# Layer 1's sums of a two-layer graph attention kernel: two column-tiled rounds in a row instead of one

## The chip, the cores and the metric

The kernel runs on one core of a Trainium2 chip. Its engines work side by side and meet at semaphores: TensorE (PE; its weight loads are a row of their own, PEld), VectorE (DVE), ScalarE (ACT), GpSimd (POOL, which here issues the gathers) and SyncE (SP, which issues most other transfers). Sixteen DMA engines move the data. The metric is the device time of one execution in microseconds (us), lower is better.

## The reference, cut to what matters

3125 nodes with 768 features each, 53,125 edges sorted by destination, two graph attention layers. The first one has 4 heads of 256 columns, the second one head of 768.

```python
h = jnp.maximum(_layernorm(x), 0.0)
def gat_conv(x, edge_index, W, a_src, a_dst, bias, heads, out_ch, concat):
    xl = (x @ W).reshape(n, heads, out_ch)
    ...
    e = jax.nn.leaky_relu(alpha_src[src] + alpha_dst[dst], 0.2)
    m = jax.ops.segment_max(e, dst, num_segments=n)
    e = jnp.exp(e - m[dst])
    s = jax.ops.segment_sum(e, dst, num_segments=n)
    alpha = e / (s[dst] + 1e-16)
    msg = xl[src] * alpha[:, :, None]
    out = jax.ops.segment_sum(msg, dst, num_segments=n)
...
h = gat_conv(x, edge_index, W1, a_src1, a_dst1, b1, HEADS, HID, True)
h = jax.nn.relu(layer_norm(h, g1, be1)) + (h0 @ Wr1 + br1)
h1 = h
h = gat_conv(h, edge_index, W2, a_src2, a_dst2, b2, 1, OUT_DIM, False)
h = layer_norm(h, g2, be2) + (h1 @ Wr2 + br2)
```

The change lies in layer 1's last sum: for each node, the rows `xl[src]` of its edges, each times its weight, added up.

## The kernel before

All is float32 in this part. The products of layer 1 are written to a table in HBM, 1024 columns (4 KB) a row. Destination nodes are worked on in 25 blocks (`NB`) of 128, the last of 53. The edges of a block lie in up to 17 tiles (`J`) of 128 slots. A tile serves one quarter of the block's nodes, 32 of them, and three tiles serve two quarters (`QUARTERS`).

`sums` (line 703) does the sum. For each tile, one indirect DMA on POOL gathers the 128 source rows into a buffer `g` (512 KB, line 774; `ahead` = 13 buffers in layer 1). DVE builds the columns `w` (lines 800 and 801): for each head a matrix of 128 slots by 32 nodes, with the edge's weight where slot and node belong together. TensorE multiplies `w` (as weights, 32 columns) with 256 columns of `g` and adds in PSUM (`pa`, line 821). A matmul with 32 columns uses a quarter of the array, and the output's quarter of the partitions says which. So tiles of different quarters are taken together: `ROUNDS` (line 33) has five rounds of 4, 4, 3, 3 and 3 tiles for a block, and within a round the four quarters follow one another for each 256 columns. Each float32 matmul is two instructions, and a round has 4 x 4 x 2 = 32. A buffer of `g` is free when its round has ended.

Between the rounds other work is done, one step after each round (`step(k)`, line 714), in this order:

- the next piece of `first()` (line 1198), which at the start finishes the totals of the weights, stores them, and loads `W2`;
- the next piece of each block that is being finished (`finish`, line 725, and `end1`, line 1207): three steps of waiting (`lag`), then normalisation on DVE and ACT, eight transposes on TensorE (line 1229), bias, gain, ReLU and residual on ACT and DVE (1234, 1236), a store of `h1T`, 12, 12 and 8 products with `W2` (line 1250) in three steps, copies of these from PSUM (1255 on ACT, 1257 on DVE) and a store to the table of layer 2. The transposes and these products share the two PSUM buffers `p2`;
- `pace[k]` pieces of `later()` (line 1170), the product `h0 @ Wr1` for 13 of the blocks in six groups. A piece is two matmuls (four instructions, line 1181); three pieces fill one `pr` buffer in PSUM (two of them), which ACT empties (line 1188). Its input `h0k` is loaded column block by column block for the next group as the last row of products of a group is done (`load`, line 1160; 11 buffers). A group waits while more than four blocks of it would stand unfinished, and for that time there are no pieces.

The order on PE, ACT and DVE is the order in which the program writes the instructions; SP and POOL take theirs as a scheduler lists them, and wait in that order for buffers. After the matmuls of a round, `fetch` (line 767) issues the next round's gathers, `w`, the load of the block's own rows (`own`, SP) and the small lookup of the totals (`ao`, POOL), and then comes the step. Layer 2 calls the same `sums` (line 1364) with one head of 768 columns and 26 buffers.

Of the kernel before, what the change touches and what calls it, by code (L numbers as in the profile page):

```python
# [9 lines left out]
F32 = mybir.dt.float32  # L10
# [58 lines left out]
def in_order(  # L69
# [16 lines left out]
    nc = tc.nc  # L86
# [5 lines left out]
    P = 128  # L92
# [23 lines left out]
    def rows_of(b):  # L116
        return P if b < NB - 1 else LAST
# [582 lines left out]
        nc.vector.tensor_scalar(ends[:, :, :, 1], al, -1.0, None, op0=OP.is_ge)  # L700
        nc.vector.scalar_tensor_tensor(ends[:, :, :, 2], eo, 2.0, ends[:, :, :, 1], op0=OP.mult, op1=OP.mult)

    def sums(heads, cols, table, al, alo_d, ahead, lag, gp, pp, end, more, pace, first=None):

        width = heads * cols
        f = width // 2
        n = min(cols, f)  # L710
        running = []
        due = 0.0

        def step(k):
            nonlocal due
            next(first or iter(()), None)
            for g in list(running):
                if next(g, running) is running:
                    running.remove(g)
            due += pace[k]  # L720
            while due >= 1.0:
                due -= 1.0
                next(more, None)

        def finish(b, own, pa):
            for _ in range(lag):
                yield

            r = rows_of(b)
            share = None  # L730
            if heads == 1:
                at = pa[:r, 1, f:f + 3]
                v = gp.tile([P, 4], F32, name="v", bufs=2)[:r]
                nc.vector.tensor_scalar(v[:, 0:1], at[:, 1:2], 0.1, 2.0, op0=OP.is_lt, op1=OP.mult)
                nc.vector.tensor_scalar(v[:, 1:2], at[:, 1:2], 0.1, None, op0=OP.max)
                nc.vector.reciprocal(v[:, 1:2], v[:, 1:2])
                nc.vector.scalar_tensor_tensor(v[:, 2:3], at[:, 2:3], v[:, 1:2], v[:, 0:1], op0=OP.mult, op1=OP.add)
                nc.vector.tensor_scalar(v[:, 3:4], at[:, 0:1], v[:, 2:3], 1e-16, op0=OP.add, op1=OP.add)
# [12 lines left out]
            for o in range(0, width, n):  # L751
                nc.vector.scalar_tensor_tensor(z[:, o:o + n], own[:r, o:o + n], aw[:r, o // cols:o // cols + 1],  # L752
                                               pa[:r, o // f, o % f:o % f + n], op0=OP.mult, op1=OP.add)
            yield from end(b, z, share)

        asked = {}

        def ask(b):
            ao = asked[b] = gp.tile([128, 2 * heads, NB], F32, name="ao", bufs=3)
            nc.gpsimd.indirect_dma_start(  # L760
                out=ao.rearrange("p v b -> p (v b)"), out_offset=None, in_=alo_d[:, :],
                in_offset=bass.IndirectOffsetOnAxis(ap=at_last[:, b:b + 1], axis=0))

        extra = 3 if heads == 1 else 0
        owns = {}

        def fetch(b, k):

            got = {}
            for j in ROUNDS[k]:  # L770
                if j >= tiles_of(b):
                    continue
                g = gp.tile([128, width + extra], F32, name="g", bufs=ahead)
                nc.gpsimd.indirect_dma_start(  # L774
                    out=g[:, :width], out_offset=None, in_=table[:, :],
                    in_offset=bass.IndirectOffsetOnAxis(ap=idx_s[:, b * J + j:b * J + j + 1], axis=0))
                if heads == 1:
                    nc.scalar.activation(g[:, width:], alo_d[:, POS[j], b, :], AF.Copy)
                got[j] = g, weights_of(b, j)
                count = PLACE[j]  # L780
                if count == 4:
                    own = owns[b] = gp.tile([128, width], F32, name="own", bufs=3)
                    load_rows(nc.sync, own, table, b)
                if heads > 1 and b == 1 and count == 11:
                    ask(0)
                if heads > 1 and b and count == (13 if tiles_of(b) == J else 5):
                    ask(b)
            return got

        def weights_of(b, j):  # L790

            c = b * J + j
            lo, hi = 32 * QUARTERS[j][0], 32 * QUARTERS[j][-1] + 32
            w = gp.tile([128, heads, hi - lo], F32, name=f"w{hi - lo}", bufs=9 if hi - lo == 32 else 3)
            if heads == 1:
                nc.vector.tensor_scalar(w[:, 0, :], iota_f[:, lo:hi], rel_s[:, c:c + 1], al[:, POS[j], 0, b:b + 1],  # L796
                                        op0=OP.is_equal, op1=OP.mult)
            else:
                oh = gp.tile([128, 64], F32, name="oh", bufs=4)[:, :hi - lo]
                nc.vector.tensor_scalar(oh, iota_f[:, lo:hi], rel_s[:, c:c + 1], None, op0=OP.is_equal)  # L800
                nc.vector.tensor_tensor(w, oh[:, None, :].to_broadcast([128, heads, hi - lo]),  # L801
                                        al[:, POS[j], :, b:b + 1].to_broadcast([128, heads, hi - lo]), OP.mult)
            return w

        with tc.manual_schedule(engines={PE, ACT, DVE}):
            ready = fetch(0, 0)
            for b in range(NB):
                pa = pp.tile([P, 2, 512], F32, name="pa", bufs=2)
                opened = set()
                last_q = (rows_of(b) - 1) // 32  # L810
                for k, js in enumerate(ROUNDS):
                    made = []
                    for j, (g, w) in ready.items():
                        for i, q in enumerate(QUARTERS[j]):
                            if q <= last_q:
                                made.append((q, w[:, :, 32 * i:32 * i + 32], g))
                    for o in range(0, width, n):
                        for q, w, g in made:
                            to = (o // f, q)
                            m = n + (extra if o + n == width else 0)  # L820
                            nc.tensor.matmul(pa[32 * q:32 * q + 32, o // f, o % f:o % f + m], w[:, o // cols, :],  # L821
                                             g[:, o:o + m], start=to not in opened, stop=False,
                                             skip_group_check=True)
                            opened.add(to)
                    if k + 1 < len(ROUNDS):
                        ready = fetch(b, k + 1)
                    elif b + 1 < NB:
                        ready = fetch(b + 1, 0)
                    step(k)
                running.append(finish(b, owns.pop(b), pa))  # L830
            k = 0
            while running:
                step(k)
                k = (k + 1) % len(ROUNDS)


    with tc.tile_pool(name="m1", bufs=1) as mp:
# [318 lines left out]
        with tc.tile_pool(name="w2", bufs=1, reuse_waits="tile") as wp, tc.tile_pool(name="e1", bufs=2, reuse_waits="tile") as ep, \  # L1156
# [3 lines left out]
            def load(i, k, q=nc.sync):  # L1160
                if i < NG:
                    n = cols_of(i)
                    t = loaded[i, k] = wp.tile([128, WIDE], F32, name="h0k", bufs=11)
                    q.dma_start(t[:, :n], h0T_d[i][:, k, :n])

            for k in range(NK1):
# [31 lines left out]
            def first():  # L1198
                nonlocal w2
                yield from totals(H, al1, alo1, alo1_d, keep1, xs1, pp, "p2", 2)  # L1200
                yield
                w2 = mp.tile([128, NK2, R2], F32, tag="W", name="w2")
                for k in range(NK2):
                    nc.sync.dma_start(w2[:, k, :C2], W2[k * 128:(k + 1) * 128, :])
                nc.vector.tensor_copy(w2[:, :, C2:], wa2)
# [51 lines left out]
                        nc.vector.tensor_copy(asad2[:r, b, :], pm[:, 384:n])  # L1257
                store_rows(nc.sync, table2, b, row)

            sums(H, C1, table1, al1, alo1_d, 13, 3, gp, pp, end1, more, (2.5, 3.8, 0, 0, 0.9), first())  # L1260


    with tc.tile_pool(name="m2", bufs=1, reuse_waits="tile") as mp, \
# [573 lines left out]
```

## Time and profile before

| what | us |
|---|---|
| three runs | 1987.45, 1987.87, 1988.3 (median 1987.87) |
| the profiled execution | 1979.75 |
| its span, from the first instruction to the last | 1977.9 |
| layer 1's sums, first and last matmul of line 821 | 514.7 and 1241 |

The profile is of one execution. A line of the groups gives the line of the kernel, the engine, the operation with output and inputs, the count, then the busy time, the mean in ns of one, and the idle time of the engine before these instructions with what ended it. A line of the timeline gives start, duration and the merged instructions, and in brackets the idle time before. The ends of matmuls are modelled, so differences between starts say more than durations. DMA share is the mean busy share of the sixteen DMA engines, and packets that overlap bring it a little above 1.

### The profile page before, as it was taken

What the parts mean: (1) busy time and instruction counts of PE and PEld (TensorE: products, weight loads), DVE (VectorE), ACT (ScalarE), POOL (GpSimd) and SP (SyncE); (2) the same over time, 40 slices, a digit from 0 to 9 for tenths busy, and PEclk for the clock granted to TensorE, in tenths of its full rate; (3) what the DMA queues carried; (4) which work ended last, traced back from release to release, by engine and by line L of the source; (5) the groups of instructions that cost most, each with busy time, mean ns of one, the idle gap of its engine ahead of it and who ended that gap; (6) DMA issues with size and microseconds to landing.
All of it is one profiled execution on the core that took longest, in us unless ns stands there. A gap on an engine that the chain in (4) does not pass through costs nothing. (4 is left out here: it accounts for less than half of the span.)

```text
span 1977.9 us, 34115 instructions
## 1 busy us (share of the span) xinstructions
PE 1805.4 (91%) x12558; PEld 985.3 (50%) x12558; DVE 1062.9 (54%) x3030; ACT 296.8 (15%) x1094; POOL 905.6 (46%) x969
## 2 busy tenths in 40 slices
PE   6999999998779999999989998878889998998886
PEld 4666665665445655655555554464333333333332
DVE  7672536888445556555665564443444443444446
ACT  1121431001202211211211121101000000000000
POOL 2000101110455666656656663006666666666663
PEclk9999999999889999999998999978999999999999
DMA  6833537872799999999999996588999999999984
GB/s 211 290 102 119 142 111 220 184 175 61 274 409 366 389 402 379 405 345 402 397 375 388 383 355 248 166 282 289 317 331 331 336 328 326 330 334 329 329 302 166
DMA packets 180978, 574.87 MB, mean 291 GB/s; under 512 B 32767, under 2 KB 54265, under 8 KB 180676
## 3 DMA queue, kind: packets, MB, share of 16 engines
q0 software_dynamic: 107472, 403.57, 57.4%
q1 hardware_dynamic: 69802, 159.43, 23.3%
q10 hardware_dynamic: 3530, 9.60, 1.2%
q8 instruction: 103, 1.69, 0.3%
q14 instruction: 71, 0.58, 0.1%
HBM read 503.27 MB, written 73.85 MB: 292 GB/s over the span
## 5 line engine op out<-in xcount | busy, mean ns | idle before, releaser
L774 POOL DMA_INDIRECT g<-table,idx_s x832 | 824.7, 991 | 511.8 <-issue 205.6
L821 PE MATMUL pa<-g,w 128*32 128x256 f32 (+2 forms) x5868 | 551.4, 430 | 91.6 <-issue 67.7
L821 PEld LDWEIGHTS pa<-g,w 128*32 128x32 f32 x5868 | 207.9, 111 | 399.5 <-issue 277.4
L1289 PE MATMUL pr<-wr,h 128*128 128x384 f32 (+1 forms) x800 | 295.7, 508 | 15.0 <-issue 14.4
L1250 PE MATMUL p<-w,h1T 128*128 128x384 f32 (+2 forms) x800 | 281.9, 499 | 4.0 <-DVE h1T L1236 2.6
L796 DVE TENSOR_SCALAR w<-iota_f,rel_s,al 128x32 f32<-128x32 f32 (+1 forms) x416 | 105.1, 321 | 311.6 <-PE pa L821 210.4
L1289 PEld LDWEIGHTS pr<-wr,h 128*128 128x128 f32 (+1 forms) x800 | 143.6, 191 | 169.3 <-issue 100.8
L1250 PEld LDWEIGHTS p<-w,h1T 128*128 128x128 f32 (+1 forms) x800 | 144.8, 189 | 127.9 <-issue 34.7
L801 DVE TENSOR_TENSOR w<-oh,al 128x128 f32<-128x128 f32 (+1 forms) x416 | 132.1, 317 | 129.2 <-PE pa L821 82.2
L924 PE MATMUL pm<-w,h0l 128*128 128x344 f32 (+1 forms) x468 | 142.5, 459 | 0.0
L1181 PE MATMUL pr<-h0k,wr 128*128 128x256 f32 (+1 forms) x576 | 140.7, 391 | 1.3 <-issue 1.3
L924 PE MATMUL pm<-w,h0g 128*128 128x344 f32 x432 | 131.0, 459 | 1.6 <-ACT h0g L903 1.6
L1059 PE MATMUL pm<-h0g,wr 128*128 128x512 f32 x288 | 131.7, 605 | 0.0
L1181 PEld LDWEIGHTS pr<-h0k,wr 128*128 128x128 f32 x576 | 105.9, 190 | 30.7 <-issue 11.8
L992 POOL DMA_DIRECT2D hot_d<-ohd x25 | 13.5, 540 | 225.3 <-DVE own L502 131.1
L800 DVE TENSOR_SCALAR oh<-iota_f,rel_s 128x32 f32<-128x32 f32 (+1 forms) x416 | 112.3, 270 | 0.3 <-issue 0.2
L924 PEld LDWEIGHTS pm<-w,h0l 128*128 128x128 f32 (+1 forms) x468 | 85.6, 187 | 45.0 <-issue 7.1
L491 ACT ACTIVATE bn_sd<-bn_mv,eps 128x1 f32<-128x1 f32 (+1 forms) x50 | 14.7, 294 | 611.6 <-DVE bn_mv L487 401.8
L924 PEld LDWEIGHTS pm<-w,h0g 128*128 128x128 f32 x432 | 81.9, 193 | 42.1 <-ACT h0g L903 1.8
L1059 PEld LDWEIGHTS pm<-h0g,wr 128*128 128x128 f32 x288 | 53.4, 193 | 56.5 <-issue 56.4
L1234 ACT ACTIVATE h1T<-p,be_c,g_c 128x128 f32<-128x128 f32 (+1 forms) x200 | 72.0, 474 | 16.7 <-PE p L1229 9.5
L551 PEld LDWEIGHTS <-ohs 128*128 128x128 bf16 x1275 | 59.7, 97 | 14.3 <-issue 14.3
(304 smaller groups left out, 1407.6 us busy)
## 6 DMA issues: line engine op xcount, KB each, us to landing
s<-slo_d SPq DMA_DIRECT2D x25, 544.0 KB
g<-table,idx_s POOLq DMA_INDIRECT x832
table<-row SPq DMA_DIRECT2D x24, 512.0 KB
own<-table SPq DMA_DIRECT2D x24, 512.0 KB
h1T_d<-h1T SPq DMA_DIRECT2D x24, 512.0 KB
h<-h1T_d SPq DMA_DIRECT2D x24, 512.0 KB
hot<-hot_d SPq DMA_DIRECT2D x25, 405.1 KB
ring<-in_x_dram SPq DMA_DIRECT2D x24, 384.0 KB
```

Source lines behind the costliest of these rows:

```text
L551: nc.tensor.matmul(q[:, j], oh[:P, o:o + 128], tabs[:, i], start=(i == 0), stop=(i == 2))
L774: nc.gpsimd.indirect_dma_start(out=g[:, :width], out_offset=None, in_=table[:, :], in_offset=bass.IndirectOffsetOnAxis(ap=idx_s[:, b * J + ...
L796: nc.vector.tensor_scalar(w[:, 0, :], iota_f[:, lo:hi], rel_s[:, c:c + 1], al[:, POS[j], 0, b:b + 1], op0=OP.is_equal, op1=OP.mult)
L800: nc.vector.tensor_scalar(oh, iota_f[:, lo:hi], rel_s[:, c:c + 1], None, op0=OP.is_equal)
L801: nc.vector.tensor_tensor(w, oh[:, None, :].to_broadcast([128, heads, hi - lo]), al[:, POS[j], :, b:b + 1].to_broadcast([128, heads, hi - ...
L821: nc.tensor.matmul(pa[32 * q:32 * q + 32, o // f, o % f:o % f + m], w[:, o // cols, :], g[:, o:o + m], start=to not in opened, stop=False, ...
L924: nc.tensor.matmul(pm[:r, :C], h0[b][:, k, :], w1[:, k, i * C:(i + 1) * C], start=(k == 0), stop=(k == NK1 - 1))
L1059: nc.tensor.matmul(pm, wr1[:, k, m * 128:(m + 1) * 128], groups[gi][:, k, :], start=(k == 0), stop=(k == NK1 - 1))
L1181: nc.tensor.matmul(pm[:, :n], wr1[:, k, m * 128:(m + 1) * 128], loaded[i, k][:, :n], start=(k == 0), stop=(k == NK1 - 1))
L1234: nc.scalar.activation(hT[:, k0 + k, :r], pt[:, k, :r], AF.Relu, bias=be1_c[:, k0 + k:k0 + k + 1], scale=g1_c[:, k0 + k:k0 + k + 1])
L1250: nc.tensor.matmul(pm[:, :n], hT[:, k, :r], w2[:, k, o:o + n], start=(k == 0), stop=(k == NK2 - 1))
L1289: nc.tensor.matmul(pm[:, :384], h1[:, k, :r], wr2[:, k, i * 384:(i + 1) * 384], start=(k == 0), stop=False)
```

## The change

`sums` gets a parameter `group`, 2 in layer 1 and 1 (as before) in layer 2. The 125 rounds stand in one list, and `group` of them are fetched before the first. After the matmuls of a round, the fetch of the round two further on is issued. The steps are kept until two rounds have been issued, and then both are done, one after the other. As a block has five rounds, the pairs are (0, 1), (2, 3), (4, 0 of the next block), (1, 2), (3, 4), and the last round stands alone. The number of buffers of a 32-column `w` goes from 9 to 10, that of `h0k` from 11 to 10; that of `g` stays at 13.

```diff
-    def sums(heads, cols, table, al, alo_d, ahead, lag, gp, pp, end, more, pace, first=None):
+    def sums(heads, cols, table, al, alo_d, ahead, lag, gp, pp, end, more, pace, first=None, group=1):
...
-            w = gp.tile([128, heads, hi - lo], F32, name=f"w{hi - lo}", bufs=9 if hi - lo == 32 else 3)
+            w = gp.tile([128, heads, hi - lo], F32, name=f"w{hi - lo}", bufs=10 if hi - lo == 32 else 3)
...
-            ready = fetch(0, 0)
-            for b in range(NB):
-                pa = pp.tile([P, 2, 512], F32, name="pa", bufs=2)
...
-                for k, js in enumerate(ROUNDS):
...
-                    if k + 1 < len(ROUNDS):
-                        ready = fetch(b, k + 1)
-                    elif b + 1 < NB:
-                        ready = fetch(b + 1, 0)
-                    step(k)
-                running.append(finish(b, owns.pop(b), pa))
+            order = [(b, k) for b in range(NB) for k in range(len(ROUNDS))]
+            ready = [fetch(*order[i]) for i in range(group)]
+            due_steps = []
+            for i, (b, k) in enumerate(order):
+                if k == 0:
+                    pa = pp.tile([P, 2, 512], F32, name="pa", bufs=2)
...
+                for j, (g, w) in ready.pop(0).items():
...
+                if i + group < len(order):
+                    ready.append(fetch(*order[i + group]))
+                due_steps.append((k, (b, owns.pop(b), pa) if k == len(ROUNDS) - 1 else None))
+                if len(due_steps) == group or i + 1 == len(order):
+                    for k_, done in due_steps:
+                        step(k_)
+                        if done:
+                            running.append(finish(*done))
+                    due_steps = []
...
-                    t = loaded[i, k] = wp.tile([128, WIDE], F32, name="h0k", bufs=11)
+                    t = loaded[i, k] = wp.tile([128, WIDE], F32, name="h0k", bufs=10)
...
-            sums(H, C1, table1, al1, alo1_d, 13, 3, gp, pp, end1, more, (2.5, 3.8, 0, 0, 0.9), first())
+            sums(H, C1, table1, al1, alo1_d, 13, 3, gp, pp, end1, more, (2.5, 3.8, 0, 0, 0.9), first(), 2)
```

More of the change, by code (lines that the diff above doesn't have):

```diff
@@ L805, in sums @@
         with tc.manual_schedule(engines={PE, ACT, DVE}):
-            ready = fetch(0, 0)
-            for b in range(NB):
-                pa = pp.tile([P, 2, 512], F32, name="pa", bufs=2)
-                opened = set()
-                last_q = (rows_of(b) - 1) // 32
-                for k, js in enumerate(ROUNDS):
[L812 to L824, printed above, removed]
-                    if k + 1 < len(ROUNDS):
-                        ready = fetch(b, k + 1)
-                    elif b + 1 < NB:
-                        ready = fetch(b + 1, 0)
-                    step(k)
-                running.append(finish(b, owns.pop(b), pa))
@@ new lines, in sums @@
+            order = [(b, k) for b in range(NB) for k in range(len(ROUNDS))]
[4 more added lines that the diff above has]
+                    pa = pp.tile([P, 2, 512], F32, name="pa", bufs=2)
+                    opened = set()
+                    last_q = (rows_of(b) - 1) // 32
+                made = []
+                for j, (g, w) in ready.pop(0).items():
+                    for i_, q in enumerate(QUARTERS[j]):
+                        if q <= last_q:
+                            made.append((q, w[:, :, 32 * i_:32 * i_ + 32], g))
+                for o in range(0, width, n):
+                    for q, w, g in made:
+                        to = (o // f, q)
+                        m = n + (extra if o + n == width else 0)
+                        nc.tensor.matmul(pa[32 * q:32 * q + 32, o // f, o % f:o % f + m], w[:, o // cols, :],
+                                         g[:, o:o + m], start=to not in opened, stop=False,
+                                         skip_group_check=True)
+                        opened.add(to)
+                if i + group < len(order):
[7 more added lines that the diff above has]
+                    due_steps = []
```

## The prediction

> **What bounds the kernel now.** I read the page first, for the share of the span that each engine is busy, then the windows over layer 1's sums.
>
> ```profile
> span 1977.9 us, 34115 instructions
> PE 1805.4 (91%) x12558; PEld 985.3 (50%) x12558; DVE 1062.9 (54%) x3030; ACT 296.8 (15%) x1094; POOL 905.6 (46%) x969
> ...
> 525.00:600.00 75.00, 56.19 (x444) 29.89 (x442) 28.81 (x87) 9.46 (x23) 45.08 (x45) 0.89 1.03 408
> 604.00:855.00 251.00, 250.40 (x2050) 149.64 (x2051) 144.44 (x481) 48.34 (x139) 151.40 (x157) 1.00 1.01 387
> 855.00:900.00 45.00, 41.30 (x320) 23.75 (x316) 28.40 (x93) 8.51 (x26) 26.04 (x28) 1.00 0.94 338
> 900.00:1020.00 120.00, 118.37 (x976) 69.86 (x964) 68.45 (x225) 21.52 (x61) 73.79 (x77) 1.00 1.01 394
> 1020.00:1062.00 42.00, 35.31 (x307) 18.22 (x306) 23.87 (x81) 7.89 (x21) 25.81 (x28) 0.92 1.00 380
> 1065.00:1190.00 125.00, 124.68 (x987) 70.29 (x986) 71.93 (x237) 23.12 (x70) 76.77 (x79) 1.00 0.99 374
> 1190.00:1215.00 25.00, 19.09 (x151) 9.08 (x150) 14.47 (x46) 4.16 (x11) 14.78 (x16) 0.86 0.97 359
> ```
>
> A windows row has start:end, length, busy time of PE, PEld, DVE, ACT, POOL, then granted clock, DMA share, GB/s. Two kinds of stretch stand there. In 604:855, 900:1020 and 1065:1190 (496 us) PE is busy all the time, 250.40 of 251.00. In 525:600, 1020:1062 and 1190:1215 it has holes and the DMA is what is late; 855:900 lies between. But the first kind is no pure PE stretch: DMA shows 1.01, and 1.03 where it is surely full. TensorE is the bound with some 2% between it and the next one.
>
> Next the order of time on PE, the layer's steady rhythm:
>
> ```profile
> 669.93 1.93 PE L821 MATMUL pa<-g,w 128*32 128x256 f32 x32
> 671.80 4.15 PE L1250 MATMUL p<-w,h1T 128*128 128x384 f32 x12
> 675.88 1.93 PE L821 MATMUL pa<-g,w 128*32 128x256 f32 x32
> 677.74 2.86 PE L1250 MATMUL p<-w,h1T 128*128 128x384 f32 x8
> 680.53 1.93 PE L821 MATMUL pa<-g,w 128*32 128x256 f32 x32
> 682.40 1.09 PE L1229 MATMUL p<-ident,z 128*128 128x128 f32 x8
> ...
> 1052.91 2.37 PE L821 MATMUL pa<-g,w 128*32 128x256 f32 x40
> ...
> 1247.70 10.65 PE L1250 MATMUL p<-w,h1T 128*128 128x384 f32 x32 [1.58 <-DVE h1T L1236]
> ```
>
> A round (32 instructions on 32 columns, four side by side, so eight groups) alternates with one dense piece.
>
> **The change, part by part.** *Joints.* Round plus twelve products take 675.88 - 669.93 = 5.95 us. The row with 40 instructions, more than one round without a dense piece between, runs 2.37 - 1.93 = 0.44 us longer for two more groups, 0.22 each: a round inside a run costs 8 x 0.22 = 1.76. Twelve and 32 products give (10.65 - 4.15) / 20 = 0.325 us each, 3.90 for twelve. Together 5.66: one round trip between the two forms costs 0.29 us, and each pair of rounds saves one. Their number where PE is the bound comes from this group of 604:1020:
>
> ```profile
> L821 PE MATMUL pa<-g,w 128*32 128x256 f32 x2336 | 145.1, 382 | 3.2 <-issue 3.2
> ```
>
> 2336 / 32 = 73 rounds in 416 us, 5.7 us each. So 604:855 has 44 rounds or 22 pairs (6.4 us), 900:1020 has 21 or 10 pairs (3.0), 1065:1190 has 22 or 11 (3.2): 12.6 us. The pairs elsewhere, some 19, wait for DMA and count nothing.
>
> *What DMA allows.* The same bytes must pass. If a stretch could only fill up to a share of 1.03, 604:855 can lose 251 x 0.02 / 1.03 = 4.9 us, 900:1020 2.3, 1065:1190 125 x 0.04 / 1.03 = 4.9. By rate instead (408 GB/s) it would be 12.9, 4.1 and 10.4, and DMA would bind nowhere. I take the share, since rounds alone are not the only traffic there (stores and narrower rows). The smaller of PE's and DMA's figure, stretch by stretch: 4.9 + 2.3 + 3.2 = 10.4 us.
>
> [...]
>
> *Gathers.* POOL's list holds only gathers and the small lookups `ao`, and both keep their order; it runs ahead until a `g` buffer comes free, and there are 13 as before. So "two rounds ahead" moves no gather on POOL; what changes is when buffers come free, six to eight in a burst instead of three or four. A pair and the next one need 14 tiles in three of five cases (rounds hold 4, 4, 3, 3, 3). The fourteenth is issued when the first round of a pair has ended, and is due when the second round of the next begins: 1.87 (second round) + about 7 (two dense pieces; one takes 5.7 - 1.87 = 3.8 on average, and the pairs meant here have shorter ones) + 1.87 = 10.7 us. How long a gather takes shows at the start:
>
> ```profile
> 519.90 0.98 POOL L774 DMA_INDIRECT g<-table,idx_s  x1 [1.23 <-DMA g<-table,idx_s]
> 521.18 0.94 POOL L774 DMA_INDIRECT g<-table,idx_s  x1 [0.30 <-issue]
> 522.42 0.93 POOL L774 DMA_INDIRECT g<-table,idx_s  x1 [0.31 <-issue]
> ...
> 528.03 0.59 PE L821 MATMUL pa<-g,w 128*32 128x256 f32 x2 [1.58 <-DMA g<-table,idx_s]
> 530.60 1.03 PE L821 MATMUL pa<-g,w 128*32 128x256 f32 x2 [1.97 <-DMA g<-table,idx_s]
> 533.14 1.46 PE L821 MATMUL pa<-g,w 128*32 128x256 f32 x9 [1.52 <-DMA g<-table,idx_s]
> ```
>
> These are round 1's last three tiles: 8.1, 9.4 and 10.7 us from issue to use, with a full queue. The tile that matters is the first of its burst and stands behind fewer. Between 0 and (8.1 to 10.7) - 10.7 = 0 that is no wait, with little left; for lost slack I take 1.5 us in all, bounds 0 and 20 (the third rival).
>
> *Steps moved.* Each step is issued after its pair. In 12 of the 25 blocks the pair is a last round and the next block's first one; the dense work after it is the last eight products of one block, a piece if one is due, then the eight transposes (L1229) of the next, which need the PSUM buffers of those products. Their emptying:
>
> ```profile
> 680.04 1.09 ACT L1255 ACTIVATE row<-p 128x384 f32<-128x384 f32 x2 [9.52 <-PE p L1250]
> 681.16 0.16 DVE L1257 COPY asad<-p 128x2 f32<-128x2 f32 x1 [2.49 <-ACT row L1255]
> ...
> L1188 ACT ACTIVATE r1l<-pr,br_c 128x128 f32<-128x128 f32 (+1 forms) x98 | 29.7, 359 | 212.0 <-PE pr L1181 125.2 <-remote 49.0 <-issue 19.1
> ```
>
> It ends at 681.32; now a round hides it. Without the round, the products would be through at 677.74 + 8 x 0.325 = 680.4, and the second four transposes wait some 0.45 us. Where the due piece closes a group of `pr`, two L1188 copies (0.36 each) stand ahead on ACT and it is about 1.6 us. Going through the steps by their pace, 6 of the 12 have no piece, 4 a harmless one, 2 the bad one: 5.9 us, and behind the transposes wait two or three pieces and the next pair. Most fall where DMA would be late anyway; I charge 2. Bounds 0 and 6.
>
> The other moved work has cover. The columns `w` of two more rounds (0.23 + 0.29 us a tile) stand before the block's vector chain on DVE, which has 144 of 251 us used and its results due a pair later; ten `w32` buffers let a pair's `w` be made once the round three or two before it is through. `own` (SP) now stands ahead of `r1t` in half of the blocks and waits only for a buffer given back two blocks ago; the stores of rows and `h1T` keep their places. With ten `h0k` buffers two of six loads wait for the group in use, but are due a pair later; if that cover went, a late load would cost one gather's time, up to 10.7 us, at most five times.
>
> *Start.* One stall does go:
>
> ```profile
> 562.56 4.97 PE L821 MATMUL pa<-g,w 128*32 128x256 f32 x32 [4.66 <-DVE w L801]
> ```
>
> The `w` of this round stood on DVE behind a copy that waited for a store; made a round earlier, it doesn't. But DMA is at 1.03 here, so I put 0, bounds 0 and -4.7.
>
> Sum: -10.4 + 1.5 + 2 = -7 us (6.9). Layer 2 keeps one round per step, so nothing there. The profiled execution took 1979.75 us for its span of 1977.9, 8.1 below the runs' median 1987.87; moved by the same 7, that is 1981.
>
> **The rivals.** *DMA has room*: PE's full 12.6 us, the pairs of 855:900 (4 x 0.29) and the start's 4.7 less the 2: -16, 1972. For it speaks 408 GB/s held for 75 us; against it the share.
>
> *DMA takes it all*: the holes move from POOL's waits to PE's waits for `g`. For it 855:900, where 338 GB/s already cost PE 3.7 us; against it 0.6 us of holes in 604:855. Change -3 to +3, 1988.
>
> *Late gathers, slower.* Place: the second round of a pair, in three of five pairs, 47 x 0.6 = 28 times counting all from 604 to 1190 but the starved part. Price: the gather's time less 10.7 us. From 0.45 us late on (12.6 / 28) the joints' saving is eaten; at 1 us late it is +28 - 12.6 = +15, or +12 with some hidden by DMA: 2000. For it: 10.7 us in a full queue, and this change fills the queue and empties it in bursts. Against: queues of 604:855 stay shorter than those at the start, as PE never waits.
>
> A pair in a starved stretch also leaves PE without dense work for longer, and the clock falls with such holes:
>
> ```profile
> 1058.00:1066.00 8.00, 7.21 (x22) 3.28 (x22) 6.97 (x21) 0.00 (x0) 4.36 (x5) 0.57 1.01 397
> ...
> 1061.62 6.08 PE L1250 MATMUL p<-w,h1T 128*128 128x384 f32 x12
> ```
>
> Twelve products took 6.08 us at 0.57 in place of 4.15. PE has 19 us of holes in 525:600 and 7 in 1020:1062 to hide this; it belongs to the slower case, as up to 2 us at each of five such places.
>
> **How the numbers follow.** Forecast 35%, DMA has room 15%, DMA takes it all 20%, late gathers 30%. I call a difference under 0.2% (4 us) no change, as a measurement of this kernel can hardly tell it. The forecast's own range is 1975 to 1985 and lies nearly all on the faster side: faster 0.50, same 0.20, slower 0.30. The range takes the first rival's 1972 and the slower one up to 2000: 1970 to 2000.
>
> **What would show it.** L821 rows of 64 instructions and about 3.7 us alternating with dense runs of 7 to 8 us; DMA share of the regular stretch at 1.02 to 1.03; PE's waits for `g` under 10 us in all; transposes waiting for `row` L1255 at some ten places. It is wrong if PE's holes between 604 and 1190 exceed 15 us, if second rounds of pairs begin with a DMA wait, or if joined rounds don't come nearer to 0.22 us a group.

## The result, and the profile after

The changed kernel took 2071.55 us in the median of 4 runs (2070.35 to 2074.12), the kernel before 1987.66 us (1985.84 to 1988.3): a ratio of 1.041, with a 95% interval of 1.0387 to 1.0432. That is 84 us slower, where 7 us faster was forecast. The profiled span is 2068.5 us in place of 1977.9.

One thing has to be known before any other number here can be read. In the six later series of runs before itself did not always take the same time: 1861 to 1864 us in three and 1977 to 1990 us in the three others, one chip (number 14) showing both. What sets the two conditions apart in the traces is when TensorE's semaphore signals arrive, so they are called **prompt** and **late** below. The first pair of runs is of the late kind. In the prompt kind the changed kernel's ratio is 1.0033. The changed kernel itself ran once in each kind: its loss of 4.1% rests on the first pair alone, and other late runs are compared with it across occasions.

The first pair, then. The windows of the changed kernel over the same stretches as before (start:end, length, busy PE, PEld, DVE, ACT, POOL, granted clock, DMA share, GB/s):

```profile
525.00:600.00 75.00, 52.18 (x429) 28.89 (x433) 28.98 (x90) 8.35 (x19) 45.15 (x43) 0.77 1.00 391
604.00:855.00 251.00, 222.77 (x1756) 140.87 (x1756) 123.64 (x412) 43.84 (x127) 130.44 (x136) 0.95 0.92 336
855.00:900.00 45.00, 39.66 (x290) 23.70 (x289) 22.70 (x74) 6.40 (x18) 24.39 (x25) 0.92 0.90 316
900.00:1020.00 120.00, 107.04 (x879) 66.86 (x878) 63.84 (x211) 20.05 (x58) 64.12 (x68) 0.96 0.95 352
```

TensorE, busy 250.40 of 251.00 us before, is busy 222.77; the clock fell from 1.00 to 0.95, and the DMA, thought to be the limit, from a share of 1.01 to 0.92. Nothing is at its limit any more: something makes everybody wait. One longer window over each kernel gives the price, before first:

```profile
604.00:1160.00 556.00, 543.06 (x4397) 316.11 (x4395) 323.74 (x1067) 103.67 (x296) 337.82 (x350) 0.99 1.00 384
```

```profile
604.00:1160.00 556.00, 492.93 (x3860) 300.99 (x3860) 281.72 (x933) 93.79 (x267) 298.52 (x309) 0.94 0.93 340
```

In the same time TensorE got through 3860 matmuls in place of 4397, which is 556 x (1 - 3860 / 4397) = 68 us of work not done. Idle time grew by 543.06 - 492.93 = 50 us. By the clock's records in the traces, TensorE lost 4.9 us of full speed while it was busy before the change and 24.6 after it, 20 us more; clock lost while it idles costs nothing by itself. The joints should have given back up to 12 (43 pairs at the predicted 0.29 us). That is 58 to 70 us in all, which covers the 68 only if the joints gave back little. The missing 84 us lie in layer 1's sums, not in layer 2: the last of the products (L1255) ends 87 us later than before's, and the kernel as a whole 91.

Where TensorE idles is in the groups of the same window (busy, mean ns | idle before, and what ended it); before and after:

```profile
L1250 PE MATMUL p<-w,h1T 128*128 128x384 f32 (+1 forms) x633 | 224.6, 500 | 1.5 <-issue 1.2
L821 PE MATMUL pa<-g,w 128*32 128x256 f32 x3136 | 200.5, 385 | 10.2 <-issue 8.0 <-DMA g<-table,idx_s 2.1
L1181 PE MATMUL pr<-h0k,wr 128*128 128x256 f32 (+1 forms) x476 | 115.8, 390 | 1.3 <-issue 1.3
L1229 PE MATMUL p<-ident,z 128*128 128x128 f32 x152 | 20.8, 280 | 0.0
```

```profile
L823 PE MATMUL pa<-g,w 128*32 128x256 f32 x2752 | 185.5, 398 | 14.2 <-issue 12.9
L1186 PE MATMUL pr<-h0k,wr 128*128 128x256 f32 (+1 forms) x428 | 111.1, 411 | 30.7 <-ACT r1l L1193 22.9 <-remote 5.4 <-issue 1.4
L1234 PE MATMUL p<-ident,z 128*128 128x128 f32 x136 | 21.9, 299 | 17.0 <-issue 15.1 <-ACT row L1260 1.5 <-DVE asad L1262 0.3
```

The rounds wait hardly longer than before. New are 30.7 us ahead of pieces, which wait for ScalarE to empty a `pr` buffer (L1193), and 17.0 us ahead of transposes. The 15.1 us put down there to "issue" are waits as well: each of these seven ends within 0.06 us of the end of a row copy (L1260) or of the small copy L1262 behind it. One of the first kind in the timeline of the changed kernel (start, duration, in brackets the idle time before and its releaser):

```profile
666.57 1.09 PE L1234 MATMUL p<-ident,z 128*128 128x128 f32 x8
667.50 3.62 PE L1186 MATMUL pr<-h0k,wr 128*128 128x256 f32 x16
667.66 0.94 POOL L774 DMA_INDIRECT g<-table,idx_s  x1 [0.30 <-issue]
...
675.13 0.94 POOL L774 DMA_INDIRECT g<-table,idx_s  x1 [0.30 <-issue]
675.89 0.63 ACT L1193 ACTIVATE r1l<-pr,br_c 128x128 f32<-128x128 f32 x2 [12.58 <-remote]
676.40 2.91 ACT L1239 ACTIVATE h1T<-p,be_c,g_c 128x128 f32<-128x128 f32 x8
676.57 4.67 PE L1186 MATMUL pr<-h0k,wr 128*128 128x256 f32 x12 [5.45 <-remote]
```

A piece is four of these instructions (0.23 us each) and a group of `pr` three pieces. The sixteen are the last piece of one group, through at about 668.5, and the three of the next. ScalarE has been idle for 12.58 us, yet its copy of the first group starts at 675.89, and only then can the third group have the buffer. ScalarE is not slow; the signal is: the group's last matmul ends at 668.53, its semaphore update is recorded at 675.86, 7.3 us later, and the copy starts 0.03 us after that. And the twelve matmuls after the stall take 4.67 us where sixteen took 3.62; the windows over that stretch have the clock, 0.50:

```profile
671.00:676.00 5.00, 0.12 (x1) 0.00 (x0) 0.00 (x0) 0.11 (x1) 3.78 (x5) 0.74 0.94 321
676.00:680.00 4.00, 3.43 (x8) 2.81 (x9) 1.34 (x3) 3.84 (x12) 0.07 (x1) 0.50 1.01 407
```

The trace also records when each semaphore was raised. Matched to TensorE's instructions over 604:1160 (each to the latest that it can belong to, so the lags are at least these), the signals that fall into a burst of gathers on POOL (less than 0.6 us apart) come a median of 2.2 us late before the change and 2.8 us after it, up to 8.5 and 9.1; outside a burst the medians are 0.12 and 0.05 us. In all traces of the prompt kind no signal is later than 0.13 us, although the bursts are longer there (5.5 gathers in the mean before the change, against 3.6). The lag was thus in the trace of before, but hardly anything waited for it. The change also made it longer where it matters: the r1l copies, which empty the `pr` buffers, started 0.9 us after their groups in the mean before and 4.4 us after the change.

### The profile page after: what moved, and what is told of

The parts are those of the page before. It is cut to its first block, busy times and chain, and to the rows that moved or that the text cites. A ratio compares the mean times of both kernels' runs of the same rounds, so it can differ in the third digit from the quotient of the medians.

```text
span 2068.5 us, 33843 instructions
## 1 busy us (share of the span) xinstructions
PE 1829.3 (88%) x12558; PEld 1009.6 (49%) x12558; DVE 1066.0 (52%) x3030; ACT 296.8 (14%) x1094; POOL 897.7 (43%) x969
## 5 line engine op out<-in xcount | busy, mean ns | idle before, releaser
L823 PEld LDWEIGHTS pa<-g,w 128*32 128x32 f32 x5868 | 218.3, 114 | 396.7 <-issue 299.6
L1255 PE MATMUL p<-w,h1T 128*128 128x384 f32 (+2 forms) x800 | 274.9, 494 | 6.9 <-issue 3.8
L1255 PEld LDWEIGHTS p<-w,h1T 128*128 128x128 f32 (+1 forms) x800 | 146.9, 188 | 123.9 <-issue 24.8
L1186 PE MATMUL pr<-h0k,wr 128*128 128x256 f32 (+1 forms) x576 | 154.1, 419 | 36.9 <-ACT r1l L1193 29.0
L1186 PEld LDWEIGHTS pr<-h0k,wr 128*128 128x128 f32 x576 | 115.5, 207 | 69.2 <-ACT r1l L1193 31.1
L997 POOL DMA_DIRECT2D hot_d<-ohd x25 | 13.5, 541 | 224.5 <-DVE own L502 128.4
L1241 DVE TENSOR_TENSOR h1T<-h1T,r1t 128x512 f32<-128x512 f32 x24 | 16.6, 692 | 142.3 <-ACT h1T L1239 119.5
```

The costliest lines, as they stand in the source:

```text
L1186: nc.tensor.matmul(pm[:, :n], wr1[:, k, m * 128:(m + 1) * 128], loaded[i, k][:, :n], start=(k == 0), stop=(k == NK1 - 1))
L1255: nc.tensor.matmul(pm[:, :n], hT[:, k, :r], w2[:, k, o:o + n], start=(k == 0), stop=(k == NK2 - 1))
```

## The experiments

In the texts written before each run, a *flip* is the eight transposes of a block, a *turn* the copies of their results into `h1T` on ScalarE, a flip stall TensorE's wait ahead of the transposes and a pr stall its wait for a `pr` buffer.

### Four edits of the changed kernel (prompt, before 1860.6 us)

The first edit undoes the joining alone:

```diff
-                if len(due_steps) == group or i + 1 == len(order):
+                if due_steps:
```

> Fetch two rounds ahead, w 10 and h0k 10 as in the changed kernel, but the steps stand after every round again, so that no two rounds touch and no dense run is doubled. Theory (the doubled dense runs expose the handover of the pr and p2 buffers through ScalarE, whose signals from TensorE come microseconds late): about the time of before, 1988 us (1980 to 1998), TensorE's wait for pr in the sums under 4 us against 36.7 now. Rival (the earlier fetch and the buffer counts do it): it stays near 2070. Rival (two rounds' gathers in one burst overload the DMA): with the fetch two ahead but the releases one round at a time again, also near 1988; this run does not tell it from the theory, the next ones do.

Measured: 1863.35 us, ratio 1.0018 (1.0002 to 1.0034).

The second spreads the pieces:

```diff
-            ... more, (2.5, 3.8, 0, 0, 0.9), first(), 2)
+            ... more, (1.44, 1.44, 1.44, 1.44, 1.44), first(), 2)
```

> The changed kernel with the pieces spread evenly, 1.44 a step (3 at most in a dense run in place of up to 7). Theory: the six pr stalls of 4.9 to 6.8 us between 604 and 1270 go, with about 3.4 us of half clock behind each: 36.7 + 6 x 1.7 us or more, so 2005 to 2030 us; the flip stalls (20 us) stay. Rival (buffers, bursts of gathers on the DMA): the same gathers in the same bursts, so the lost time turns up at another wait and it stays within 15 us of 2070.

Measured: 1866.74 us, ratio 1.0025 (1.0003 to 1.0047).

The third regroups the products:

```diff
-                    if k in (2, 5, 7):
+                    if k == 3:
                         yield
```

> The changed kernel with the products of a block in two halves of 16 (third and fourth step after the turn starts) in place of 12, 12 and 8, so that the row copies and the next block's transposes are a pair of rounds apart. Theory: the seven flip stalls of 1.3 to 3.5 us (20 us) go, with some half clock behind them (up to 12 us); the pr stalls stay: 2040 to 2055 us. Rival: within 10 us of 2070.

Measured: 1995.79 us, ratio 1.0723 (1.0692 to 1.0754). The fourth holds both of these edits.

> Both edits in one kernel: pieces 1.44 a step, products in two halves of 16. Theory: both kinds of stall gone, so that what is left is the gain of the joints that the changed kernel already has (some 18 us of the sums): 1970 to 1990 us, at or below before. Rival (buffers, bursts): 2040 or more.

Measured: 1961.11 us, ratio 1.0546 (1.0525 to 1.0568). Both are misses. The group of the third kernel in 604:1160:

```profile
L1234 PE MATMUL p<-ident,z 128*128 128x128 f32 x136 | 26.1, 355 | 50.0 <-DVE oh L800 38.6 <-DVE z L1227 11.4
```

The transposes now wait 50.0 us in a window of 556 us, for VectorE: the eight products that stood ahead of them in the pair (4, next 0) were not their obstacle but their cover, under which VectorE finished normalising `z` (L1227, queued behind the `oh` of the rounds fetched ahead). This cover is read from the releasers and the order of the instructions; no run restores it alone. The rounds wait another 31.2 us there, 25.6 of them for VectorE's `z` (L752), and the fourth kernel's transposes 47.6 us. The theory's flip stalls were read rightly as a wait and wrongly as a wait that moving the products would end.

### The changed kernel again, and long runs without joints (prompt, before 1860.54 us)

The first two results could not be read without the changed kernel on the same chip.

> The changed kernel once more, beside before on the same chip. In the first pair of traces TensorE's signals reached ScalarE late in the sums (the r1l copy started 4.05 us after its group's end in the mean); in the four traces of the first experiments, on another chip, the signals came within 0.1 us. Theory A (the late signals are the cause of the pr and flip stalls): where signals are prompt the changed kernel has under 5 us of waits for pr and runs within 1% of before (ratio 0.995 to 1.010); where they are late, 1.041 again. Rival B (the handover stalls at the normal time of a copy too): 1.04 on any chip, with the pr waits of 30 us and more.

Measured: 1866.09 us, ratio 1.0033 (1.0017 to 1.0049).

> Before's own profile on this chip, to compare with. Theory A: the ratio is 1.0 by construction; the sums of layer 1 last 720 to 760 us and the lag of TensorE's signals is that of the chip, the same as in the changed kernel's trace beside it (median under 0.1 us, or over 1 us in the bursts of gathers).

Measured: 1862.62 us in one run. Their windows, before first:

```profile
604.00:1160.00 556.00, 550.51 (x4524) 322.68 (x4513) 329.91 (x1089) 109.32 (x312) 349.80 (x364) 1.00 1.01 397
```

```profile
604.00:1160.00 556.00, 542.69 (x4566) 332.56 (x4565) 332.14 (x1090) 108.87 (x315) 347.20 (x362) 1.00 1.01 395
```

and the changed kernel's groups:

```profile
L823 PE MATMUL pa<-g,w 128*32 128x256 f32 x3264 | 195.8, 382 | 9.8 <-DMA g<-table,idx_s 9.8
L1186 PE MATMUL pr<-h0k,wr 128*128 128x256 f32 (+1 forms) x501 | 120.6, 391 | 0.4 <-DMA h0k<-h0T_d 0.4
L1234 PE MATMUL p<-ident,z 128*128 128x128 f32 x160 | 23.1, 281 | 3.1 <-ACT row L1260 2.4
```

With prompt signals the wait for `pr` is 0.4 us, so a copy's normal time never delays a third group. TensorE needs 8 us less for slightly more matmuls, which are the joints, and then waits 9.8 us for gathers. Both kernels stand at the same DMA share, 1.01.

```diff
-            ... more, (2.5, 3.8, 0, 0, 0.9), first())
+            ... more, (7.2, 0, 0, 0, 0), first())
```

> Before, rounds apart, with all of a block's pieces in one step (7.2 after the first round in place of 2.5, 3.8 and 0.9): runs of seven pieces without any joining of rounds. Theory A: where signals are prompt, within 1% of before (a copy of 0.5 us is done long before the third group); where they are late, a pr stall in most blocks, 20 to 80 us slower. Rival B: slower by 30 us or more on any chip.

Measured: 1858.66 us, ratio 0.9997 (0.998 to 1.0014). Runs of seven pieces cost nothing where signals are prompt.

> The changed kernel with 1.44 pieces in every step, again, beside the changed kernel itself on one chip. Theory A: no pr stalls on any chip; where signals are late it beats the changed kernel by 40 us or more, where they are prompt by under 15 us. Rival B: it beats the changed kernel by 40 us on either.

Measured: 1867.66 us, ratio 1.0028 (1.001 to 1.0046), the same as the changed kernel within the intervals.

### Copies made late on purpose (late, before 1977.27 us)

Meant for the prompt condition, as a stand-in for the lag; the runs fell into the late one, so the delay came on top of the lag.

```diff
                             if k == NK1 - 1:
+                                idle = wp.tile([P, 640], BF16, name="idle")
+                                nc.scalar.activation(idle[:, :1], pm[:P, :1], AF.Copy)
+                                for _ in range(9):
+                                    nc.scalar.activation(idle, b1_b[:, :640], AF.Copy)
                                 for t, b in enumerate(members):
```

> The changed kernel with its r1l copies made late on purpose: after a group of pieces ends, ScalarE first does nine idle copies of 640 elements (about 6.8 us, from the 731 ns of one such copy in the profile of before), then the r1l copies. That is about the lag of 7 us that TensorE's signals had at the big pr stalls of the first trace of the changed kernel. Theory A (lateness of ScalarE, exposed by six and seven pieces in a run, is the loss): six to eight pr stalls of 4 to 5 us between 604 and 1190, half clock behind each, and the ratio to before 1.02 to 1.045. Rival C (the loss on the first chip was something else that chip does, and the late signals only went with it): within 1% of the changed kernel on this kind of chip, ratio 1.00 to 1.01.

> The same nine idle copies before the r1l copies in the kernel before (h0k 10 in place of 11 to make room). Theory A: the runs of pieces are two to four long, a third group starts only after another round of 5.7 us, so the same lateness costs little: ratio 1.00 to 1.012, waits for pr under 12 us in the sums. Rival D (the lateness stalls any kernel, the joints have no part): the ratio is that of the joined kernel with the delay, within 1%.

> The changed kernel with 1.44 pieces in every step and the same nine idle copies. Theory A: three pieces at most in a dense run, so no third group waits for the first's copy within it: waits for pr under 12 us, ratio 1.00 to 1.012. Rival D: 1.02 or more, as the joined one.

Measured: joined 1.0836 (1.0778 to 1.0895), apart 1.0441 (1.0383 to 1.0498), even 1.09 (1.0846 to 1.0954). The waits of pieces for `pr` in 604:1160, joined, then apart, then the even kernel with its products and transposes:

```profile
L1186 PE MATMUL pr<-h0k,wr 128*128 128x256 f32 x424 | 119.5, 436 | 74.2 <-ACT r1l L1197 67.2 <-issue 7.0
```

```profile
L1181 PE MATMUL pr<-h0k,wr 128*128 128x256 f32 x408 | 116.2, 436 | 36.1 <-ACT r1l L1192 28.4 <-ACT idle L1189 4.6 <-issue 3.1
```

```profile
L1186 PE MATMUL pr<-h0k,wr 128*128 128x256 f32 x408 | 109.2, 410 | 5.9 <-ACT idle L1192 5.9
L1259 PE MATMUL p<-w,h1T 128*128 128x384 f32 x448 | 170.2, 531 | 44.4 <-issue 27.5 <-DVE h1T L1245 16.8
L1238 PE MATMUL p<-ident,z 128*128 128x128 f32 x112 | 21.4, 342 | 47.9 <-ACT row L1264 35.8 <-issue 5.3 <-ACT idle L1194 3.7
```

A delay of the copies does stall the joined kernel twice as long as the unjoined one (74.2 against 36.1 us), and spreading the pieces does take that wait away (5.9). But the kernel with no `pr` wait is no faster: its products and transposes wait instead, the latter for ScalarE's row copies, which now stand behind the idle copies. The expected 1.00 to 1.012 for the unjoined and the even kernel were both wrong, and so was the 1.02 to 1.045 for the joined one; on top of the lag, 6.8 us was a cost for any kernel. The run shows that the handover can stall, not that it is the whole loss.

### Long runs again, and half the bytes (prompt, before 1863.96 us)

> The changed kernel with 1.44 pieces in every step, a third time, since the chips differ: on some TensorE's signals come within 0.1 us, on others microseconds late. Theory A: on a late chip the six pr stalls are gone and the ratio falls from 1.041 to 1.00 to 1.02; on a prompt chip 1.002 to 1.005 as before. Rival D (on a late chip every handover stalls, the length of the runs of pieces has little part): 1.035 or more on a late chip.

> Before with all of a block's 7.2 pieces in one step, rounds apart, a second time for the same reason. Theory A: on a late chip a pr stall of 1 to 5 us in most blocks with seven pieces, ratio 1.01 to 1.04 without any joint; on a prompt chip 1.00. Rival E (it takes the joint: two rounds' signals and gathers in one burst make the lag): within 0.5% of before on a late chip too.

Measured: 1.0044 (1.0028 to 1.006) and 0.9978 (0.9965 to 0.9991), prompt once more. The other two kernels gather half rows, and so leave out half of each row's columns:

```diff
+                part = width if heads == 1 else width // 2
                 nc.gpsimd.indirect_dma_start(
-                    out=g[:, :width], out_offset=None, in_=table[:, :],
+                    out=g[:, :part], out_offset=None, in_=table.rearrange("n (t c) -> (n t) c", c=part),
...
-                                         g[:, o:o + m], ...
+                                         g[:, o % part:o % part + m], ...
```

> The changed kernel with gathers of half a row in layer 1 (512 of 1024 columns, every matmul reads that half; as many gathers, half their bytes). On a prompt chip: the sums are no longer bound by the DMA, so the 66 joints show what they save, and this kernel beats its apart twin by 10 to 18 us. On a late chip: if the lag comes from GpSimd's work on the gathers (1.24 us each whatever their bytes), signals in the bursts stay late (median over 1.5 us) and the joined kernel stays 2 to 4% behind its apart twin; if it comes from the DMA's traffic, the median lag falls under 0.7 us and the two are within 1%.

> Before with the same gathers of half a row, the twin of the run ahead. On a prompt chip: DMA share in the sums about 0.6, and 10 to 18 us slower than the joined twin. On a late chip: lag as before's (median 2.4 us in the bursts) if GpSimd's work makes it, under 0.7 us if the traffic does.

Measured: joined 1834.06 us (1833.2 to 1835.56), apart 1840.33 us (1837.17 to 1842.96). Their windows, joined first:

```profile
604.00:1130.00 526.00, 521.68 (x4473) 322.32 (x4472) 321.58 (x1054) 108.45 (x312) 345.17 (x357) 1.00 0.75 242
```

```profile
604.00:1130.00 526.00, 525.59 (x4378) 309.74 (x4380) 319.84 (x1043) 105.39 (x300) 340.24 (x349) 1.00 0.75 238
```

With the DMA at 0.75 the joined kernel is faster, by 6.3 us; the profiled sums differ by 12 us (691.5 against 703.4), the spans of the same two executions by 7.4. The joints do save time. Halving the bytes is all that was changed in both kernels, so that the saving vanishes at a share of 1.01 is put down to the DMA. 6.3 is under the 10 to 18 expected: the joined kernel keeps 3.1 us of waits of transposes, and layer 1 has 62 pairs, not the 66 written there. The share of 0.75 is above the 0.6 expected.

### Even pieces in the late condition (before 1990.11 us)

> The changed kernel with 1.44 pieces in every step, once more, for the condition with late signals (before near 1980 us). Theory A there: waits for pr under 8 us in the sums (36.7 in the changed kernel), the flip stalls stay, and the ratio is 1.00 to 1.025. Rival D (the joints stall at the next handover whatever the pieces): 1.03 or more. In the prompt condition (before near 1862 us) 1.002 to 1.005 again, which tells nothing new.

Measured: 2059.2 us, ratio 1.0369 (1.0317 to 1.042). The `pr` waits are gone as foreseen, the time is not:

```profile
L823 PE MATMUL pa<-g,w 128*32 128x256 f32 x2790 | 207.3, 398 | 37.2 <-issue 35.3
...
L1186 PE MATMUL pr<-h0k,wr 128*128 128x256 f32 (+1 forms) x428 | 104.3, 383 | 0.0
L1234 PE MATMUL p<-ident,z 128*128 128x128 f32 x136 | 19.9, 282 | 8.8 <-ACT row L1260 4.9 <-issue 3.5 <-DVE asad L1262 0.4
```

```profile
604.00:1160.00 556.00, 510.27 (x3930) 312.05 (x3930) 292.05 (x965) 92.98 (x265) 306.91 (x317) 0.97 0.94 349
```

37.2 us now stand ahead of rounds, and the DMA share is 0.94, nearly as low as the changed kernel's 0.93. One such pair of rounds:

```profile
731.77 1.33 PE L823 MATMUL pa<-g,w 128*32 128x256 f32 x11
733.90 0.64 PE L823 MATMUL pa<-g,w 128*32 128x256 f32 x4 [0.80 <-issue]
735.35 1.09 PE L823 MATMUL pa<-g,w 128*32 128x256 f32 x4 [0.81 <-issue]
737.49 0.38 PE L823 MATMUL pa<-g,w 128*32 128x256 f32 x1 [1.04 <-issue]
738.18 4.50 PE L823 MATMUL pa<-g,w 128*32 128x256 f32 x44 [0.32 <-issue]
```

A pair that should take 3.66 us takes 10.9. "Issue" is right here: the instructions after the pauses wait for no semaphore at all, and the same holds for 34.3 of the 35.3 us that TensorE idles in gaps over 0.15 us ahead of round instructions. Rival D is borne out: the joints lose nearly as much whatever the pieces, and the first theory, that the long runs of pieces are the loss, falls.

Such pauses can be counted: two successive TensorE instructions inside rounds, weight loads included, whose starts lie 0.45 us or more apart, the later one without a semaphore to wait for. In 604:1160 there are none in any prompt trace. In the late condition before has 18 (13.0 us), the changed kernel 38 (25.2 us) and the one with even pieces 86 (63.3 us), against 17 (13.5 us) and 4 (3.5 us) in the two unjoined kernels below. Their median is 0.7 us. They do not coincide with loads of instructions: with even pieces only 8 of the 86 overlap one of the 31 transfers of the instruction queue q8 (16 KB each) in that window.

### Joining undone, and fewer buffers (late, before 1977.64 us)

> The changed kernel with the steps after every round (joining undone, all its buffer counts and the fetch two ahead kept). Theory F (in the late condition it is the joining: two rounds' signals and eight gathers in one burst, five spare g buffers): late condition (before near 1980 us): ratio 0.995 to 1.010, DMA share in the sums back to 1.00; prompt condition (before near 1862 us): 1.000 to 1.004 as in the first run. Rival G (the fetch two ahead or the smaller h0k and larger w counts): 1.03 or more in the late condition.

Measured: 1975.92 us, ratio 0.9996 (0.997 to 1.0021). In its window the DMA share is back at 1.00:

```profile
604.00:1160.00 556.00, 541.67 (x4361) 314.92 (x4361) 321.23 (x1058) 104.28 (x298) 335.96 (x351) 0.99 1.00 384
```

So the 4.1% of the first pair come with the joining, as far as two late occasions can be compared; the fetch two ahead and the buffer counts cost nothing that shows (0.997 to 1.0021).

```diff
-            sums(H, C1, table1, al1, alo1_d, 13, 3, ...
+            sums(H, C1, table1, al1, alo1_d, 9, 3, ...
```

> Before, unjoined, with 9 g buffers in place of 13: a round holds 4, so 5 are spare, as many as beside the 8 of a joined pair. Theory F, late condition: the gathers start late and the DMA's share falls to 0.90 to 0.96, ratio 1.02 to 1.06; prompt condition: 1.000 to 1.015. If spare buffers have no part (the burst alone counts): within 0.5% of before in either condition.

Measured: 1984.85 us, ratio 1.0036 (1.0013 to 1.0058), DMA share 0.99. Five spare buffers are enough when rounds are released one at a time, so that number alone is not the cause either. A pair, though, holds its buffers for two rounds; that was not tried apart.

## Why the prediction was wrong, point by point

The step that failed is what the joined steps were charged: 2 us under *Steps moved*, and nothing for the rest ("The other moved work has cover"). In the late condition the joining cost 84 us: with the steps back after every round and all else kept, the ratio is 0.9996 in place of 1.041. Through which effect it costs that stays open, as the end of this section says. The gain that was set against it, 10.4 us for the joints, did not come at full bytes even in the prompt condition. The prediction's own sign of being wrong, over 15 us of holes on TensorE, was met: 63 us in 604:1160 alone.

*Joints.* Right. A joined pair of rounds takes 3.66 us undisturbed, as forecast ("about 3.7"), and with DMA to spare (a share of 0.75) the joined kernel wins.

```profile
716.69 3.66 PE L823 MATMUL pa<-g,w 128*32 128x256 f32 x64
```

0.29 us a pair was somewhat high for the net: 6.3 us over 62 pairs are 0.10 a pair by the medians, 12 us or 0.19 by the profiled sums.

*What DMA allows.* The step "if a stretch could only fill up to a share of 1.03" failed, even without the lag: with prompt signals before already stands at 1.01 and so does the changed kernel, and the term of -10.4 us bought nothing: the whole change came to +6 us there (0.33% of 1861). The rival "DMA takes it all" names what happens; its change of -3 to +3 us was near, though below the interval (3 to 9 us). The 408 GB/s that spoke for room came from a stretch in which TensorE idled; over 556 us of the prompt traces before moves 397 and the changed kernel 395.

*Gathers, "for lost slack I take 1.5 us in all, bounds 0 and 20".* Mis-sized in the late condition. The DMA share fell by 0.07 over the regular part, about 40 us in 556. It does not show as TensorE's waits for `g`, which the prediction named as its test, since TensorE stood before pieces and transposes meanwhile. The slower rival chose the right side but not the mechanism: second rounds did not begin with a DMA wait.

*Flips, charged 2 us (bounds 0 and 6).* 17.0 us in the 556 us window of the late trace, 3.1 in the prompt one. The working assumed a row copy that starts when the products end. In the late condition its signal comes late: in six of the nine stalls of 0.7 us or more the first row copy starts 1.6 to 3.5 us after the products' end. The row quoted for L1188 said as much: 49.0 us of ScalarE's idle time there were ended by something "remote", and the prediction did not ask what.

*"The other moved work has cover."* This is where the costliest wait was left out. The `pr` buffers, two of them, are also handed over inside a dense run, and a run twice as long has six or seven pieces, so that a third group needs what ScalarE must first empty. At a copy's normal pace that is free (0.4 us, prompt); with signals 7 us late it is 30.7 us. It was not costed at all. It is not a price to add to the others, as the even pieces show.

*The clock.* Put down as "up to 2 us at each of five such places" in the slower rival alone; while TensorE was busy it took 20 us more than before in 556 us, as stalls like the one shown are followed by a stretch at half speed: the windows have 0.50 in 676:680, after the stall of 5.45 us. In the clock's records of the changed kernel such a stretch lasts 6.8 us at each of the six stalls of 4.9 to 6.8 us for `pr` between 604 and 1270; it begins within the stall and reaches 2.85 to 6.07 us past its end.

What is shown: the loss comes with the joining (0.9996 without it against 1.041, both late, on two occasions), and it is that large only where signals come late (1.0033 where they don't). What is not settled is through which of its effects. The `pr` handover and the flips carry it in the changed kernel; with even pieces nearly the same time is lost in pauses inside the rounds, so these waits are not to be added up as independent costs. A common cause behind both is likely but not shown. What makes a condition late stays open as well.

## What to carry to other kernels

A schedule that interleaves two kinds of work also gives every handover between engines time to happen (in 604:1160 the pieces waited 1.3 us before the change and 30.7 after it, both late); before closing the gaps, list each buffer that is passed on inside the longer run, and price its signal at the lag the trace shows, not at the copy's duration. That alone would not have saved this change: with the costliest handover out of the way the kernel was still 3.7% slower. Where a resource already stands at a share of 1.00 in the regular stretch, ask whether work saved on another engine can buy anything; here it bought nothing (1.01 in both prompt kernels, ratio 1.0033). And take a second run on another occasion before explaining a loss: here the same edit is worth 0.3% or 4%.

## What the runs showed of the hardware that was not expected

The same kernel has two conditions, 6 to 7% apart, one of them seen on a chip that on another occasion showed the other. In the late one TensorE's signals arrive up to 9 us late while GpSimd works through gathers, TensorE pauses for 0.7 us at a time ahead of instructions that wait for nothing, and the sums of layer 2 take 609 us in place of 527; GpSimd's own time for a gather is the same in both (967 and 963 ns in the sums of layer 1). The DMA engines move less at nearly the same share: 384 GB/s at 1.00 against 397 at 1.01 over 604:1160.

The traces differ in one more way. All eight late ones have lost about 40% of their semaphore records (17,100 updates in the trace of before, 29,285 in its prompt one), of TensorE's own some 5%; the prompt ones have lost hardly any. Matmuls and DMA packets are complete in both. Whether the lost records are a cause of the lag or another effect of the same thing, no run here shows, and as every run here comes with a recorded clock and span, none tells what a kernel does without a recording.

The pauses counted above stand inside rounds, where TensorE starts 64 instructions, weight loads counted, in 1.9 us, and there were more of them when two rounds were joined: 38 in place of 18 in the first pair, 86 with even pieces, 17 and 4 in the two unjoined kernels of the late condition. What causes them no run here shows.
